# A graph layer on one core: layers in five parts, later merging, and 16 chunks loaded row by row instead of 21

## The chip, the cores and the metric

The kernel runs on one core of a Trainium2 chip. The metric is the time of one execution on the device in microseconds; lower is better. The core's engines work side by side, each through its own queue: PE multiplies matrices, DVE and ACT do elementwise work, POOL issues the indirect gathers, and SP (and in the set-up ACT) issues the plain transfers.

## The reference

One block of a graph network: normalise the rows of x, take the mean of the source rows over the edges that end at each node, and send mean and own row through four dense layers.

```python
h = jnp.maximum(_layernorm(x, axis=-1), 0.0)           # x: (12500, 128)
msgs = h[src]                                          # src, dst: (200000,), sorted by dst
agg = jax.ops.segment_sum(msgs, dst, num_segments=n)
deg = jax.ops.segment_sum(ones, dst, num_segments=n)
agg = agg / jnp.maximum(deg, 1.0)[:, None]
y = jax.nn.relu(agg @ Wg + h @ Ws + bg)                # 128
y = jnp.tanh(y @ W1 + b1)                              # 512
y = jnp.tanh(y @ W2 + b2)                              # 512
return x + (y @ W3 + b3)                               # 128
```

All of it is float32; the input has its edges sorted by dst.

## The kernel before

The program first normalises x in pieces of up to 14 x 128 rows and stores the result, the table `htab`, in HBM (lines 162 to 234). Meanwhile POOL gathers 80 chunks of rows straight from x ("raw" chunks, line 141), since the table isn't there yet; they are normalised later, eight at a time.

A chunk is 128 edges, 1563 chunks in all. For each, the 128 source rows must come into SBUF, and PE multiplies them with a one-hot matrix (which edge belongs to which node of a window of 56 to 160 nodes), adding up in PSUM: this is an add (`add`, line 413). There are three ways for the rows to come in:

- the 80 raw chunks, ten groups of eight, every 40 chunks from chunk 256 on;
- 1462 chunks by one indirect DMA each, issued by POOL (`gather`, line 296), into a ring of 32 buffers (`AHEAD`);
- 21 chunks row by row: SP reads each row's address into a register and issues a plain DMA of 512 bytes (`row_loads`, line 315). `slow` lists these chunks: from `SLOW0` = 72 up to `QUICK` = 1376, after each one `EACH` = 58 others that are not raw. They come in batches of 16 rows, a batch for every 58 x 16 / 128 = 7.25 gathered chunks, into two buffers. For each such chunk `places` (line 307) loads its 128 indices and DVE multiplies them by the length of a row, one chunk ahead.

The nodes are cut into blocks: 23 of 512, one of 256, three of 128 and one of 84. Blocks that share chunks have these added into a tensor of their own (`edge`), which is merged into both blocks' sums by a matmul with the identity (`merge`, line 437). Two chunks behind the last chunk of a block, `merge` runs and the block's layers start.

`layers` (line 498) is a generator; each `next` emits a matmul or so. Up to chunk `QUICK` the main loop (line 586) takes one step of the oldest block's layers every two chunks. From there on the order is timed: `there` (line 612) is a chunk's due time, 12.0 + 1.25 us for each gather, and before each add all steps are emitted that fit ahead of it; `soonest` (line 568) chooses between the two oldest blocks. PE's order is the program's order: `pe` and `sp_dma` keep what they issue in place.

The own rows of a block, `hb`, and x, `xb`, are loaded by `own` (line 460) some 50 chunks ahead; `own_turned` transposes `hb`. Sums, layers and x end in `o`, which SP stores `LATE` = 12 chunks later.

Of the kernel before, what the change touches and what calls it, by code (L numbers as in the profile page):

```python
# [22 lines left out]
F32 = mybir.dt.float32  # L23
BF16 = mybir.dt.bfloat16
I32 = mybir.dt.int32
U8 = mybir.dt.uint8
AF = mybir.ActivationFunctionType
ALU = mybir.AluOpType
# [10 lines left out]
RAW0 = 256  # L39
STEP = 40  # L40
AHEAD = 32
SLOW0 = 72
EACH = 58
LOADS = 16
LATE = 12
QUICK = 1376

WINDOWS = ((0, 144), (1496, 88), (1536, 56))
# [9 lines left out]
def windowed(ctx, tc, x, src, dst, Wg, Ws, bg, W1, b1, W2, b2, W3, b3, out, flag):  # L58
# [20 lines left out]
    def raw(c):  # L79
        return RAW0 <= c < RAW1 and (c - RAW0) % STEP < GRP  # L80


    slow, n = [], 0
    for c in range(SLOW0, QUICK):
        if not raw(c):
            if n == 0:
                slow.append(c)
                n = EACH
            else:
                n -= 1  # L90
# [202 lines left out]
    def sp_dma(*a):  # L293
        tc.keep_in_program_order(nc.sync.dma_start(*a))  # L294

    def gather(c):
# [4 lines left out]
        )  # L301
        rows_t[c] = r

    ROWB = 4 * D
    hbytes = htab.rearrange("n d -> (n d)").bitcast(U8)

    def places(c):

        ix = ed.tile([1, P], I32, name="ix", bufs=2)
        sp_dma(ix, src[c * P : (c + 1) * P].rearrange("(o p) -> o p", o=1))  # L310
        at = ed.tile([1, P], I32, name="at", bufs=2)
        nc.vector.tensor_scalar(at, ix, float(ROWB), None, op0=ALU.mult)
        return at

    def row_loads():
        nxt_at = places(slow[0])
        for i, c in enumerate(slow):
            at = nxt_at
            if i + 1 < len(slow):
                nxt_at = places(slow[i + 1])  # L320
            r = rows_one.tile([P, D], F32, name="srows")
            rows_t[c] = r
            rb = r.bitcast(U8)
            for p0 in range(0, P, LOADS):
                loads, vs = nc.values_load_multi_w_load_instructions(
                    at[:, p0 : p0 + LOADS], engines=[mybir.EngineType.SP], min_val=0, max_val=(N - 1) * ROWB,
                    skip_runtime_bounds_check_because="src holds rows of x, as the indirect DMAs take it to",
                )
                for ld in loads:
                    tc.keep_in_program_order(ld)  # L330
                for p, v in enumerate(vs, p0):
                    sp_dma(rb[p : p + 1, :], hbytes[bass.ds(v, ROWB)].rearrange("(o b) -> o b", o=1))
                yield
# [126 lines left out]
    def own(s):  # L460

        n0 = s * BLK
        n = min(BLK, N - n0)
        k, whole = -(-n // P), n // P
        xb = ml.tile([P, BLK // P, D], F32, name="xb", bufs=3)
        if whole < k:
            nc.vector.memset(xb[:, whole, :], 0.0)
        if whole:
            sp_dma(xb[:, :whole, :], x[n0 : n0 + whole * P, :].rearrange("(t p) d -> p t d", p=P))
        if whole < k:  # L470
            sp_dma(xb[: n - whole * P, whole, :], x[n0 + whole * P : n0 + n, :])
        hb = ml.tile([P, BLK // P, D], F32, name="hb", bufs=1)
        sp_dma(hb[:, :k], htab[n0 : n0 + k * P, :].rearrange("(t p) d -> p t d", p=P))
        owns[s] = (hb, xb)

    def own_turned(s):

        k = -(-min(BLK, N - s * BLK) // P)
        hb, xb = owns.pop(s)
        pt = ps_t.tile([P, BLK // P, P], F32, name="pt")  # L480
        for t in range(k):
            pe.transpose(pt[:, t, :], hb[:, t, :], ident)
        hT = ml.tile([P, BLK], F32, name="hT")
        nc.scalar.copy(hT[:, : k * P], pt[:, :k, :].rearrange("p t n -> p (t n)"))
        hTs[s] = (hT, xb)

    def own_part(b):

        n0, n = blocks[b]
        whole = n // P  # L490
        xb = ml.tile([P, -(-n // P), D], F32, name=f"xs{b}", bufs=1)
        if whole:
            sp_dma(xb[:, :whole, :], x[n0 : n0 + whole * P, :].rearrange("(t p) d -> p t d", p=P))
        if n > whole * P:
            sp_dma(xb[: n - whole * P, whole, :], x[n0 + whole * P : n0 + n, :])
        xss[b] = xb

    def layers(b):


        n0, n = blocks[b]
        s, off = divmod(n0, BLK)
        hT, xb = hTs[s]
        k, whole = -(-n // P), n // P
        rest = n - whole * P
        if n != BLK:
            xb = xss.pop(b)
        mm, hop = 4 * (n / 2400 + 0.003), 0.5 + n / 1200

        size, bufs = (P, 2) if n <= P else (BLK, 1)  # L510
        yield 0, 0
        mT = ml.tile([P, BLK], F32, name="mT")
        nc.vector.tensor_tensor(mT[:, :n], acc[b][:, :n], rds.pop(b)[:, :n], op=ALU.mult)  # L513
        yield mm, 0
        p0 = flat(ps_m.tile([P, 4, P], F32, name="pm"))
        pe.matmul(p0[:, :n], ws, hT[:, off : off + n], start=True, stop=False)
        yield mm, n / 90
        pe.matmul(p0[:, :n], wg, mT[:, :n], start=False, stop=True)
        h0 = ml.tile([P, BLK], F32, name="h0")
        nc.scalar.activation(h0[:, :n], p0[:, :n], AF.Relu, bias=bgc)  # L520
        yield 0, 0
        h1 = ml.tile([P, HM, size], F32, name=f"h1_{size}", bufs=bufs)
        for m in range(HM):
            yield mm, hop if m == 0 else 0
            p1 = flat(ps_m.tile([P, 4, P], F32, name="pm"))
            pe.matmul(p1[:, :n], w1[:, m * P : (m + 1) * P], h0[:, :n], start=True, stop=True)
            nc.scalar.activation(h1[:, m, :n], p1[:, :n], AF.Tanh, bias=b1c[:, m : m + 1])  # L527
        h2 = ml.tile([P, HM, size], F32, name=f"h2_{size}", bufs=bufs)
        for m in range(HM):
            p2 = flat(ps_m.tile([P, 4, P], F32, name="pm"))  # L530
            for kk in range(HM):
                yield mm, hop if m == 0 and kk == HM - 1 else 0
                pe.matmul(
                    p2[:, :n], w2[:, kk, m * P : (m + 1) * P], h1[:, kk, :n], start=(kk == 0), stop=(kk == HM - 1)
                )
            nc.scalar.activation(h2[:, m, :n], p2[:, :n], AF.Tanh, bias=b2c[:, m : m + 1])  # L536
        p3 = flat(ps_m.tile([P, 4, P], F32, name="pm"))
        for kk in range(HM):
            yield mm, hop if kk == HM - 1 else 0
            pe.matmul(p3[:, :n], w3[:, kk, :], h2[:, kk, :n], start=(kk == 0), stop=(kk == HM - 1))  # L540
        h3 = ml.tile([P, BLK], F32, name="h3", bufs=1)
        nc.scalar.activation(h3[:, :n], p3[:, :n], AF.Identity, bias=b3c)  # L542
        yield 0, 0
        yield k * 0.225, hop
        po = ps_t.tile([P, BLK // P, P], F32, name="pt")
        for t in range(k):
            r = min(P, n - t * P)
            pe.transpose(po[:r, t, :], h3[:, t * P : t * P + r], ident)
        o = ml.tile([P, BLK // P, D], F32, name="o")
        if whole:  # L550
            nc.vector.tensor_tensor(o[:, :whole], po[:, :whole], xb[:, :whole], op=ALU.add)
            stores.append((at, out[n0 : n0 + whole * P, :].rearrange("(t p) d -> p t d", p=P), o[:, :whole, :]))
        if rest:
            nc.vector.tensor_tensor(o[:rest, whole], po[:rest, whole], xb[:rest, whole], op=ALU.add)
            stores.append((at, out[n0 + whole * P : n0 + n, :], o[:rest, whole, :]))

    order = [c for c in range(NCH) if not raw(c) and c not in slow]
    loading = row_loads()
    work, done, nxt, behind = [], 0, 0, 0
# [6 lines left out]
            sp_dma(*stores.pop(0)[1:])  # L566

    def soonest():
        two = work[: 2 if len(work) > 1 and work[1][3] < work[0][3] else 1]
        return min(two, key=lambda w: max(w[2], now), default=None)  # L570

    def go_on(w):
        nonlocal now
        if w:
            now = max(now, w[2]) + w[1]
            w[1:] = *next(w[0], (None, 0)), w[3] + 1
            w[2] += now
            if w[1] is None:
                work.remove(w)
# [6 lines left out]
    for c in range(NCH):  # L586
# [22 lines left out]
                next(loading, 0)  # L609
        if c >= QUICK:  # L610

            there = 12.0 + 1.25 * (NRAW * GRP + order.index(c)) if c not in slow else 0
            while soonest() and max(now, soonest()[2]) < there:
                go_on(soonest())
            now = max(now, there) + 0.27
        add(c)

        if done < len(blocks) and (c - 2 if across[done] else c) == reach[done][-1]:
            if across[done]:
                merge(done)  # L620
            work.append([layers(done), 0, 0, 0])
            done += 1
        if (c // span + 1) * BLK < N:
            if c % span == span - 52:
# [389 lines left out]
```

## Time and profile before

| | us |
|---|---|
| median of 3 runs | 1955.35 (1953.97 to 1955.7) |
| profiled execution | 1952.27 |
| its span | 1950.5 |
| POOL busy | 1458.0 (75%) |
| PE busy | 1354.8 (69%) |
| DVE busy | 1069.7 (55%) |
| ACT busy | 231.8 (12%) |

The profile is that of one execution, with times from the start of its span. A group of instructions shows the line, the engine, the operation, the tile written and those read, the count, the busy time with the mean of one, and the engine's idle time ahead of them with what ended it. "issue" stands for time in which the engine waited for nothing that the profile shows. The records name line 285, 288 or 294 for all of PE's edge and layer matmuls, transposes and SP's plain DMAs, since helpers issue them; the tile names tell them apart. A float32 matmul appears as two records.

### The profile page before, as it was taken

To read this page: it belongs to the slowest core of one execution; us is meant where nothing else is said; L and a number is where in the kernel's file an instruction comes from. 1 tells how busy PE (TensorE), PEld (TensorE's weight loads), DVE (VectorE), ACT (ScalarE), POOL (GpSimd) and SP (SyncE) were. 2 spreads that over 40 slices of the span, in tenths; PEclk is the share of its full clock that TensorE was granted. 3 is DMA by queue.
4 is the path that set the end of the run, shared out by engine and by line. 5 is a ranking of instruction groups with operands and counts; after the bars stand their busy time and mean duration, and the time that the engine had idled before them with its cause. 6 is when DMAs were issued, how large, how long until landed. Compare 5 with 4: busy or idle time off the path is not lost.

```text
span 1950.5 us, 20753 instructions
## 1 busy us (share of the span) xinstructions
PE 1354.8 (69%) x5213; PEld 803.5 (41%) x5213; DVE 1069.7 (55%) x671; ACT 231.8 (12%) x364; POOL 1458.0 (75%) x1550
## 2 busy tenths in 40 slices
PE   0057387778787787776676677677776676778797
PEld 0034253444454444433333334343343343454466
DVE  7874874655666566645445445455455454545430
ACT  1100211101111011101011001010110101101122
POOL 7777777777777777777777777777777777777774
PEclk9999689899899989999999998989889889868797
DMA  7822222222222222222222222222222222222221
GB/s 199 231 77 65 54 70 54 70 65 60 71 70 71 64 60 70 70 54 71 70 54 70 54 71 70 54 71 65 60 70 54 71 70 53 77 69 61 55 63 38
DMA packets 125595, 139.78 MB, mean 72 GB/s; under 512 B 33169, under 2 KB 99958, under 8 KB 125272
## 3 DMA queue, kind: packets, MB, share of 16 engines
q0 software_dynamic: 49344, 101.16, 20.5%
q1 hardware_dynamic: 72962, 33.90, 6.3%
q10 hardware_dynamic: 3160, 3.31, 0.6%
q8 instruction: 43, 0.70, 0.2%
q14 instruction: 86, 0.70, 0.1%
HBM read 125.43 MB, written 12.82 MB: 71 GB/s over the span
## 4 chain that ended last, share of the span: by engine, by line
issue 36%; DMA 26%; PE 24%; POOL 11%; DVE 1%; ACT 0%; SPq 0%; POOLq 0%; DVEq 0%; ACTq 0%
DMA rows<-htab,scol 26%; PE pm L285 12%; PE agg L285 8%; POOL rows L298 7%; POOL raw L141 4%; PE edge L285 3%; PE pt L288 1%; DVE oh L362 0%; DVE shared L171 0%; DVE raw L172 0%; DVE shared L175 0%; ACT sq L174 0%; DMA raw<-in_x_dram,rsrc 0%; SPq L294 0%; DVE rd L399 0%
## 5 line engine op out<-in xcount | busy, mean ns | idle before, releaser
L298 POOL DMA_INDIRECT rows<-htab,scol x1462 | 1379.5, 944 | 445.8 <-issue 293.4
L285 PE MATMUL agg<-oh,rows 128*128 128x144 f32 (+3 forms) x2096 | 543.9, 358 | 331.5 <-DMA rows<-htab,scol 327.7
L285 PEld LDWEIGHTS agg<-oh,rows 128*128 128x128 f32 x2096 | 369.4, 217 | 711.4 <-DMA rows<-htab,scol 595.0
L285 PE MATMUL pm<-h,w 128*128 128x512 f32 (+3 forms) x1344 | 614.1, 553 | 0.2
L362 DVE TENSOR_TENSOR oh<-shared,dloc 128x1152 f32<-128x1152 f32 (+2 forms) x186 | 245.2, 1322 | 622.5 <-PE agg L285 420.3
L372 DVE TENSOR_REDUCE cnt<-oh 128x200 bf16<-128x1600 f32 (+2 forms) x186 | 523.6, 2825 | 7.9 <-DMA htab<-h 3.6
L285 PE MATMUL edge<-oh,rows 128*128 128x144 f32 (+2 forms) x828 | 211.9, 347 | 131.3 <-DMA rows<-htab,scol 130.4
L285 PEld LDWEIGHTS edge<-oh,rows 128*128 128x128 f32 x828 | 139.8, 206 | 264.6 <-DMA rows<-htab,scol 216.9
L285 PEld LDWEIGHTS pm<-h,w 128*128 128x128 f32 x1344 | 212.7, 197 | 11.8 <-issue 9.8
L536 ACT ACTIVATE h<-pm,b2c 128x512 f32<-128x512 f32 (+3 forms) x112 | 70.8, 632 | 649.1 <-PE pm L285 649.1
L141 POOL DMA_INDIRECT raw<-in_x_dram,rsrc x80 | 77.6, 970 | 25.5 <-issue 23.8
L527 ACT ACTIVATE h<-pm,b1c 128x512 f32<-128x512 f32 (+3 forms) x112 | 70.2, 632 | 182.1 <-PE pm L285 181.5
L399 DVE RECIPROCAL rd<-rd 128x512 f32<-128x512 f32 (+3 forms) x28 | 81.8, 2920 | 0.0
L513 DVE TENSOR_TENSOR mT<-agg,rd 128x512 f32<-128x512 f32 (+3 forms) x28 | 17.3, 619 | 90.5 <-PE agg L285 90.5
L200 PE MATMUL pm<-ident,idx_f 98*128 98x98 f32 x32 | 6.2, 376 | 76.3 <-DVE agg L179 42.7
L285 PE MATMUL agg<-sums,ident 128*128 128x140 f32 (+3 forms) x108 | 28.4, 412 | 27.5 <-ACT sums L427 27.5
L397 DVE TENSOR_SCALAR rd<-pm 128x512 f32<-128x512 f32 (+3 forms) x28 | 17.4, 621 | 52.4 <-PE pm L285 52.4
L520 ACT ACTIVATE h<-pm,bgc 128x512 f32<-128x512 f32 (+3 forms) x28 | 17.7, 632 | 236.4 <-PE pm L285 236.4
L542 ACT ACTIVATE h<-pm,b3c 128x512 f32<-128x512 f32 (+3 forms) x28 | 17.7, 632 | 184.5 <-PE pm L285 184.5
L285 PE MATMUL pm<-hT,ws 128*128 128x512 f32 (+3 forms) x56 | 38.6, 784 | 0.0
L285 PEld LDWEIGHTS agg<-sums,ident 128*128 128x128 f32 x108 | 25.4, 309 | 28.3 <-ACT sums L427 28.3
L200 PEld LDWEIGHTS pm<-ident,idx_f 98*128 98x128 f32 x32 | 5.1, 223 | 77.1 <-issue 42.9
(70 smaller groups left out, 497.4 us busy)
## 6 DMA issues: line engine op xcount, KB each, us to landing
srows<-htab SPq DMA_DIRECT2D x2688, 0.5 KB
rows<-htab,scol POOLq DMA_INDIRECT x1462
xb<-in_x_dram SPq DMA_DIRECT2D x24, 256.0 KB
hb<-htab SPq DMA_DIRECT2D x24, 256.0 KB
out_dram<-o SPq DMA_DIRECT2D x23, 256.0 KB
htab<-h SPq DMA_DIRECT2D x6, 896.0 KB
xt<-in_x_dram SPq DMA_DIRECT2D x5, 896.0 KB
raw<-in_x_dram,rsrc POOLq DMA_INDIRECT x80
```

The source lines that it names most:

```text
L141: nc.gpsimd.indirect_dma_start(out=t[:, j, :], out_offset=None, in_=x, in_offset=bass.IndirectOffsetOnAxis(ap=rsrc[:, g, j : j + 1], axis=0),)
L285: tc.keep_in_program_order(nc.tensor.matmul(*a, **k))
L288: tc.keep_in_program_order(nc.tensor.transpose(*a, **k))
L298: nc.gpsimd.indirect_dma_start(out=r, out_offset=None, in_=htab, in_offset=bass.IndirectOffsetOnAxis(ap=scol[:, c : c + 1], axis=0),)
L362: nc.vector.tensor_tensor(oh[:, :k, :w], lane[:, None, :w].to_broadcast([P, k, w]), dloc[:, g * GRP : g * GRP + k][:, :, None].to_broadcas ...
L372: nc.vector.tensor_reduce(cnt[:, :n], shifted, AX.X, ALU.add)
L397: nc.vector.tensor_scalar(rd[:, :m], dg[:, :m], 1.0, None, op0=ALU.max)
L399: nc.vector.reciprocal(rd[:, :m], rd[:, :m])
L520: nc.scalar.activation(h0[:, :n], p0[:, :n], AF.Relu, bias=bgc)
L527: nc.scalar.activation(h1[:, m, :n], p1[:, :n], AF.Tanh, bias=b1c[:, m : m + 1])
L536: nc.scalar.activation(h2[:, m, :n], p2[:, :n], AF.Tanh, bias=b2c[:, m : m + 1])
L542: nc.scalar.activation(h3[:, :n], p3[:, :n], AF.Identity, bias=b3c)
```

## The change

- **Layers in parts.** `layers` is split into `part0` (mean, first layer), `part1` and `part2` (the two tanh layers), `part3` (last matmul) and `part4` (transposes, adding x, store). For blocks whose layers start before `QUICK`, `part3` and `part4` of a block run within the next block's: `part0(b)`, `part3(b-1)`, `part1(b)`, `part4(b-1)`, `part2(b)`.
- **Merging.** Up to `QUICK` a block is merged, and its layers start, 10 chunks (`LEAD`) behind its last chunk instead of 2; after that 2 as before.
- **Row loads.** `SLOW0` goes from 72 to 160, `EACH` from 58 to 80, and the list ends at chunk 1462 instead of 1375. That makes 16 chunks (160, 241, ... 1375), and a batch of 16 rows for every 10 gathered chunks.
- **Their offsets.** The indices of all 16 chunks are loaded in the set-up by 16 DMAs on ACT's queue into 16 partitions and multiplied by one DVE instruction; `places` goes away.
- **x.** `own` loads only `hb`; x is loaded by `own_part` when a block's layers start.
- **The timed order.** The due time is 7.5 + 1.251 us for each gather; the second oldest block is chosen only if the oldest is one of the last small ones (`w[4]`).

```diff
-SLOW0 = 72
-EACH = 58
+SLOW0 = 160
+EACH = 80
 LOADS = 16
 LATE = 12
+LEAD = 10
 QUICK = 1376
...
-    for c in range(SLOW0, QUICK):
+    for c in range(SLOW0, NCH - 100):
...
-    def places(c):
-
-        ix = ed.tile([1, P], I32, name="ix", bufs=2)
-        sp_dma(ix, src[c * P : (c + 1) * P].rearrange("(o p) -> o p", o=1))
-        at = ed.tile([1, P], I32, name="at", bufs=2)
-        nc.vector.tensor_scalar(at, ix, float(ROWB), None, op0=ALU.mult)
-        return at
+    at_i = const.tile([len(slow), P], I32, name="at_i")
+    for i, c in enumerate(slow):
+        nc.scalar.dma_start(at_i[i : i + 1, :], src[c * P : (c + 1) * P].rearrange("(o p) -> o p", o=1))
+    place = const.tile([len(slow), P], I32, name="place")
+    nc.vector.tensor_scalar(place, at_i, float(ROWB), None, op0=ALU.mult)
...
     def row_loads():
-        nxt_at = places(slow[0])
         for i, c in enumerate(slow):
-            at = nxt_at
-            if i + 1 < len(slow):
-                nxt_at = places(slow[i + 1])
...
-                    at[:, p0 : p0 + LOADS], engines=[mybir.EngineType.SP], min_val=0, max_val=(N - 1) * ROWB,
+                    place[i : i + 1, p0 : p0 + LOADS], engines=[mybir.EngineType.SP], min_val=0, max_val=(N - 1) * ROWB,
...
+    def one_by_one(*parts):
+        for part in parts:
+            yield from part()
+
+    def layers(b, before):
+
+
+        part = lambda f, *a: lambda: f(*a)
+        last = [] if before is None else [part(part3, before), part(part4, before)]
+        if reach[b][-1] + LEAD < QUICK:
+            return one_by_one(
+                part(part0, b), *last[:1], part(part1, b, True), *last[1:], part(part2, b)
+            )
+        return one_by_one(
+            *last, part(part0, b), part(part1, b, False), part(part2, b), part(part3, b), part(part4, b)
+        )
...
     def soonest():
-        two = work[: 2 if len(work) > 1 and work[1][3] < work[0][3] else 1]
+        two = work[: 2 if len(work) > 1 and work[1][3] < work[0][3] and work[0][4] else 1]
...
-            there = 12.0 + 1.25 * (NRAW * GRP + order.index(c)) if c not in slow else 0
+            there = 7.5 + 1.251 * (NRAW * GRP + order.index(c)) if c not in slow else 0
...
-        if done < len(blocks) and (c - 2 if across[done] else c) == reach[done][-1]:
+        lead = LEAD if c < QUICK else 2
+        if done < len(blocks) and (c - lead if across[done] else c) >= reach[done][-1]:
             if across[done]:
                 merge(done)
-            work.append([layers(done), 0, 0, 0])
+            quick = reach[done][-1] + LEAD >= QUICK
+
+            before = done - 1 if done and reach[done - 1][-1] + LEAD < QUICK else None
+            work.append([layers(done, before), 0, 0, 0, quick and blocks[done][1] <= P])
             done += 1
```

The bodies of the five parts are those of the old `layers`, cut at these places; `part0` calls `own_part` for a block of 512, and `part1` gives two empty steps more before `QUICK`.

## The prediction

> **What bounds the kernel now.** I read the groups of the page first, then POOL's own waits, then the timeline at both ends of POOL's gathers.
>
> ```profile
> L298 POOL DMA_INDIRECT rows<-htab,scol x1462 | 1379.5, 944 | 445.8 <-issue 293.4
> L285 PE MATMUL agg<-oh,rows 128*128 128x144 f32 (+3 forms) x2096 | 543.9, 358 | 331.5 <-DMA rows<-htab,scol 327.7
> L285 PE MATMUL edge<-oh,rows 128*128 128x144 f32 (+2 forms) x828 | 211.9, 347 | 131.3 <-DMA rows<-htab,scol 130.4
> ```
>
> POOL issues 1462 gathers of 944 ns and is idle 445.8 us between them; PE sits idle some 460 us ahead of its adds, waiting for gathered rows. Whether POOL ever waits for something is told by the longest wait of each kind (last column):
>
> ```profile
> POOL rows L298 <- issue: 293.4, 962, 0.3
> POOL rows L298 <- PE agg L285: 61.0, 200, 0.3
> POOL rows L298 <- DMA rows<-htab,scol: 35.4, 116, 0.3
> POOL rows L298 <- PE edge L285: 27.1, 89, 0.3
> ```
>
> None is over 0.3 us, whatever engine it is booked to: this is the fixed gap of a gather (445.8 / 1462 = 0.305 us), not a stall. So the page's 75% busy POOL is saturated. The two ends of the row of gathers, on POOL's timeline:
>
> ```profile
> 103.70 0.94 POOL L141 DMA_INDIRECT raw<-in_x_dram,rsrc  x1 [0.30 <-issue]
> 104.94 0.95 POOL L298 DMA_INDIRECT rows<-htab,scol  x1 [0.30 <-issue]
> ...
> 1928.98 0.94 POOL L298 DMA_INDIRECT rows<-htab,scol  x1 [0.31 <-POOLq L980]
> ```
>
> (1928.98 - 104.94) / 1461 = 1.2485 us for a gather, and the 80 raw gathers run straight into the first table gather. The kernel is POOL from 2.95 to 1928.98, then a tail of 1950.5 - 1928.98 = 21.5 us. A chunk of 128 edges that SP loads row by row costs POOL nothing; a gathered one costs 1.2485 us.
>
> **The count of gathers (on the path).** There are 1563 chunks (200000 / 128), 80 raw. Before, from chunk 72 to 1375 there are 1304 - 80 = 1224 that are not raw; one of 59 is row-loaded, 21 in all, so 1563 - 80 - 21 = 1462, as the page counts. After, from 160 to 1462 there are 1303 - 80 = 1223; one of 81 is row-loaded, 16 in all, so 1467. Five more gathers: 5 x 1.2485 = +6.24 us, on the engine that never waits.
>
> **What is taken from SP and DVE.** SP issues 5 x 128 = 640 fewer row DMAs, 21 fewer index loads and 40 fewer register loads (168 to 128). Sixteen row DMAs took 5.65 us of SP at 107.67, so a batch now fills 5.65 of 10 x 1.2485 = 12.5 us instead of 5.65 of 7.25 x 1.2485 = 9.1. Does POOL speed up? From 1300 to 1610, with row loads running, its gathers stand 1.2483 us apart; from 1630 to 1930, after the last row load at 1619, also 1.2483. So 0. The first two row chunks fill both buffers either way; later a batch waits for the add that frees its buffer, and behind it on SP queue x, table and output transfers. Each chunk is loaded 80 gathers ahead of its add by program order (160 - 80) where it was 14 (72 - 58): 100 us of cover against 17.5. Nothing.
>
> DVE loses 21 multiplies:
>
> ```profile
> L312 DVE TENSOR_SCALAR at<-ix x21: 158/204/370, 106.0 to 1497.1; 1x128 int32<-1x128 int32 x21
> 106.20 0.99 POOL L298 DMA_INDIRECT rows<-htab,scol  x1 [0.30 <-issue]
> 29.18 1.21 DVE L196 CAST idx_f<-idx_raw 98x2048 f32<-98x2048 int32 x1
> 29.32 1.90 POOL L141 DMA_INDIRECT raw<-in_x_dram,rsrc  x1 [0.30 <-issue]
> ```
>
> The gather beside the first two multiplies took 0.99 instead of 0.94; no other of the 1462 is above that (its longest is 990 ns). One wide multiply comes instead, beside a raw gather: 0.05 gone, 0.05 back, at most its 0.2 us. I take 0. The cast does cost the gather beside it 0.96 us; both casts stay. The Trainium skill, SBUF — State Buffer, section "SBUF: two separate sides", says that a VectorE operation in a two-port mode locks GpSimd out for the whole instruction. If that held for the multiplies too, their removal would save 21 x 0.217 = 4.6 us and the sum would be +1.6 instead of +6.2; the row of the cast fits the rule, the row of the multiplies doesn't, and the row decides.
>
> **Set-up.** ACT's queue gets 16 DMAs more, behind b3c. The eight bias loads before them began 0.52 us apart (28.71 to 32.37), so 16 x 0.52 = 8.3 us. Eleven stand ahead of the square that started at 37.81 with 5.1 us of empty queue before it: 11 x 0.52 = 5.7, so it is 0.6 late; five stand after it, 2.6 us beside its 1.70 us and the 2.17 us that ACT then waited for DVE. Behind them queue the dst index load and the next factors, and DVE's wide multiply waits for all 16. That is between 0 and 8.3 - 5.1 = 3.2 us late; if the last five also wait for a store of 640 KB (the last table store took from 93.2 to 98.1, 4.9 us), 8.1. The cover:
>
> ```profile
> 98.17 0.50 SPq L294 DMA_DIRECT2D hb<-htab  x1
> ```
>
> This load needs the whole table, which is there by 98.1; the first gather starts at 104.94 because POOL is still at raw gathers. So 6.8 us of lateness cost nothing, and the worst is 8.1 - 6.8 = +1.3. DVE, 60.5 of 63 us busy from 30 to 93, sets the end of the table; in the changed order three one-hots of 1.35 us come behind its last piece, which gives 4 us back. I take 0.
>
> **Layers in five parts, merge 10 chunks ahead.** The matmuls, tanhs and transposes are the same in number; only their places among the adds change, in the stretch where PE idles for rows. That makes PE wait less for ACT, and then wait longer for rows: 0. The cover is the ring of 32 row buffers, 32 x 1.2485 = 40 us: POOL is held only when PE falls that far behind. The longest stretch of layers without an add stands where the timed order starts, at chunk 1376: 36 records, 15.6 us (1698.48 to 1714.1). In the changed order some 42 records stand there, 15.6 x 42 / 36 = 18.2 us. Even at half clock this is 36.4, under 40. x is now loaded a block ahead of its use; no one waits.
>
> **The tail.** Behind the last wide blocks, the changed PE order is the same as before, matmul for matmul, over the last 25 adds and all layers of blocks 25 to 27 among and behind them: the constants 7.5 and 12.0 shift all due times alike. So I carry 21.5 us over. Its bounds:
>
> ```profile
> 1931.43 0.49 PE L285 MATMUL agg<-oh,rows 128*128 128x44 f32 x2
> 1934.28 0.30 PE L285 MATMUL agg<-oh,rows 128*128 128x28 f32 x2
> 1934.62 0.24 DVE L513 TENSOR_TENSOR mT<-agg,rd 128x84 f32<-128x84 f32 x1 [9.00 <-PE agg L285]
> 1943.91 0.29 DVE L554 TENSOR_TENSOR o<-pt,xs 84x128 f32<-84x128 f32 x1 [6.12 <-PE pt L288]
> ```
>
> Then busy time of PE, PE's loads, DVE, ACT and POOL in stretches of 2 us, with the granted clock behind them:
>
> ```profile
> 1920.00:1922.00 2.00, 0.84 (x4) 0.59 (x4) 0.00 (x0) 0.00 (x0) 1.46 (x2) 1.00 0.18 43
> 1922.00:1924.00 2.00, 0.85 (x7) 0.70 (x6) 0.26 (x2) 0.24 (x1) 1.39 (x3) 0.50 0.21 55
> ...
> 1930.00:1932.00 2.00, 2.00 (x11) 2.00 (x11) 0.00 (x0) 0.33 (x1) 0.00 (x0) 0.50 0.13 33
> 1932.00:1934.00 2.00, 2.00 (x18) 2.00 (x18) 0.00 (x0) 0.73 (x2) 0.00 (x0) 0.94 0.00 0
> ```
>
> A gather's rows reach PE 2.54 us after its start (the chain's commonest piece), the last ones at 1931.5; the last add ran at 1934.28, since PE was at half clock from 1922 to 1932. With PE in time the tail loses 2.8 us at most. The other way: at half clock to the very end, PE's 11.2 us of work from 1932 to 1944 would take up to 11 longer; both half-clock stretches (1902 to 1911.8, 1922 to 1932) ended some 7.5 us after PE was dense, so I take 0, and 2 for the range (4 us more at half speed). The Trainium skill, TensorE: Matmul & The Clock Gate, section "Part 1: The HAM clock gate (the "warmup" mystery)", gives a free-running window of 3.4 us; by an estimate from that page 6.24 us of shift could move the change of clock by a window, 1.7 us of work either way. Here half clock went on for 7 us after PE was dense (1904.1 to 1911.8).
>
> **Sum.** The profiled execution took 1952.27 us (span 1950.5 and 1.8 around it); 1952.27 + 6.24 = 1958.5. The median of the runs is 1955.35, 3.1 above it: 1955.35 + 6.24 = 1961.6, +0.32%. I call 0.2% (3.9 us) the least that a measurement of this kernel can tell from no change.
>
> **Rivals.**
> - The tail gives it back: better timed, PE reaches the last add with its rows. Price up to -2.8 us, 1958.8; it decides from 6.24 - 3.9 = 2.3 us on, not slower then. For it speaks the 2.8 us lag of the last add; against it the order of matmuls, unchanged there. 0.12.
> - Set-up or ring becomes the bound: the table lands after the last raw gather, or PE falls 40 us behind. +1.3 by the first, some us by the second, 1963 to 1966. Against both the covers above, 6.8 us and 22 us. 0.06.
> - The change doesn't do it by gathers: lighter SP and DVE make each gather shorter, so that 1467 of them take less. Faster needs (6.24 + 3.9) / 1467 = 0.007 us off each of them; the two equal intervals of 1.2483 speak against it. 1951.5 or less. 0.04, of which 0.03 faster.
> - The forecast, 1961.6: 0.78.
>
> Slower: 0.78 + 0.06 = 0.84. Same: 0.12 + 0.01 = 0.13. Faster: 0.03. The range runs from the tail's bound, 1958.5, to the set-up's 1.3 and the clock's 2 above the forecast with a us for the spread of runs, 1966.
>
> **What would show it.** Right: 1467 gathers in the groups, no wait of POOL over 0.3 us, first table gather at 105, last at 1935.2, and 21.5 us behind it. Wrong: a gap on POOL ahead of the first table gather (set-up), waits of POOL for PE over 0.3 us (ring), another interval than 1.2485 (rate), or a tail away from 21.5 us.

## The result and the profile after

| | before | after |
|---|---|---|
| median of 8 runs, us | 1955.34 (1953.97 to 1956.59) | 1960.88 (1960.20 to 1961.69) |
| ratio, with its 95% interval | | 1.0028 (1.0017 to 1.0039) |
| profiled execution, us | 1952.27 | 1961.69 |
| its span | 1950.5 | 1959.5 |
| gathers by POOL | 1462 | 1467 |
| first, last table gather starts at | 104.94, 1928.98 | 104.73, 1938.59 |
| from the last gather to the end | 21.5 | 20.9 |

The change costs 5.54 us, 0.28%; the interval of the ratio, 1.0017 to 1.0039, leaves out 1. One slip in the section on the change: the 16 row-loaded chunks run from 160 to 1455, not to 1375, since the raw chunks between them are skipped in the count.

The groups of the page of after first; the columns are those of the groups shown of before:

```profile
L299 POOL DMA_INDIRECT rows<-htab,scol x1467 | 1387.6, 946 | 447.5 <-issue 269.3
L286 PE MATMUL agg<-oh,rows 128*128 128x144 f32 (+3 forms) x2096 | 560.2, 365 | 335.2 <-DMA rows<-htab,scol 324.3
```

Five gathers more, and PE still idles 335 us ahead of the adds of `agg`, for rows. POOL's waits of after, with the longest of each kind last:

```profile
POOL rows L299 <- issue: 269.3, 883, 0.3
POOL rows L299 <- PE agg L286: 74.4, 244, 0.3
POOL rows L299 <- DMA rows<-htab,scol: 47.9, 157, 0.3
POOL rows L299 <- PE edge L286: 29.3, 96, 0.3
```

None is longer than the fixed gap of 0.3 us: POOL runs through, as before. The ends of its row of gathers, on POOL's timeline:

```profile
103.48 0.95 POOL L142 DMA_INDIRECT raw<-in_x_dram,rsrc  x1 [0.31 <-issue]
104.73 0.95 POOL L299 DMA_INDIRECT rows<-htab,scol  x1 [0.30 <-DVE cnt L367]
...
1938.59 0.95 POOL L299 DMA_INDIRECT rows<-htab,scol  x1 [0.30 <-POOLq L1014]
```

(1938.59 - 104.73) / 1466 = 1.2509 us a gather, against 1.2485 before. Over 1466 intervals this is 3.5 us, over half of what the five gathers cost; the two profiles by themselves therefore differ by 9.0 us of span where the medians differ by 5.5. Whether the 1.2509 belongs to the change had to be asked with a second execution (below: it doesn't). The eight timed runs of before lie 3.1 us above its profiled one in the median (1955.34 against 1952.27), close to these 3.5 us, so the slower pace may have held for both kernels in the timed runs; no profile shows it.

### The profile page after: what moved, and what is told of

It is laid out like the page before. It is cut to its first block, busy times and chain, and to the rows that moved or that the text cites. A ratio compares the mean times of both kernels' runs of the same rounds, so it can differ in the third digit from the quotient of the medians.

```text
span 1959.5 us, 19291 instructions
## 1 busy us (share of the span) xinstructions
PE 1393.8 (71%) x5213; PEld 824.1 (42%) x5213; DVE 1068.2 (55%) x650; ACT 231.8 (12%) x364; POOL 1465.9 (75%) x1555
## 4 chain that ended last, share of the span: by engine, by line
DMA 36%; issue 28%; PE 26%; POOL 7%; DVE 3%; ACT 0%; SPq 0%; ACTq 0%; POOLq 0%; DVEq 0%
DMA rows<-htab,scol 34%; PE pm L286 13%; PE agg L286 9%; POOL rows L299 7%; PE edge L286 3%; DMA xt<-in_x_dram 2%; PE pt L289 1%; DMA at_i<-in_src_dram 0%; DVE oh L357 0%; DVE agg L176 0%; DVE h L183 0%; DVE agg L172 0%; DVE xt L173 0%; DVE cnt L367 0%; DVE shared L176 0%
## 5 line engine op out<-in xcount | busy, mean ns | idle before, releaser
L286 PE MATMUL agg<-oh,rows 128*128 128x144 f32 (+3 forms) x2096 | 560.2, 365 | 335.2 <-DMA rows<-htab,scol 324.3
L286 PEld LDWEIGHTS agg<-oh,rows 128*128 128x128 f32 x2096 | 381.9, 223 | 714.1 <-DMA rows<-htab,scol 597.5
L286 PE MATMUL pm<-h,w 128*128 128x512 f32 (+3 forms) x1344 | 639.0, 573 | 1.1 <-ACT h L515 0.7
L286 PEld LDWEIGHTS edge<-oh,rows 128*128 128x128 f32 x838 | 145.0, 210 | 277.1 <-DMA rows<-htab,scol 242.3
L286 PEld LDWEIGHTS pm<-h,w 128*128 128x128 f32 x1344 | 219.8, 202 | 15.2 <-issue 12.0
L564 DVE TENSOR_TENSOR o<-pt,xb 128x512 f32<-128x512 f32 x23 | 15.9, 690 | 95.7 <-PE pt L289 91.9
L472 ACT COPY hT<-pt 128x512 f32<-128x512 f32 (+1 forms) x25 | 14.4, 578 | 258.5 <-PE pt L289 246.9
L289 PE MATMUL pt<-ident,hb 128*128 128x128 f32 x98 | 16.6, 297 | 31.5 <-DMA srows<-htab 31.5
```

The source lines that it names most:

```text
L286: tc.keep_in_program_order(nc.tensor.matmul(*a, **k))
L289: tc.keep_in_program_order(nc.tensor.transpose(*a, **k))
```

## The experiments

The experiments ran on three chips, and each is compared only with the kernel before on its own chip. There before took 2498.71 us (first group below), 1951.77 (second group; 1951.51 beside the last run, on the same chip) and 1952.18 (third group). The chip of the first group is slower, SP's queue among the rest, for a cause that stays open.

### On a slow chip

*again* is the kernel before, unchanged, for its profile on this chip.

> The kernel before, unchanged, for its trace beside the others. After the change a gather took 1.2509 us in the profile, before it 1.2485. If the change makes gathers slower, this run shows 1.2485 again and the change's 1466 intervals hold 3.5 us that the count doesn't explain. If the two executions differ as a whole, it shows 1.250 to 1.251 here, with raw gathers at the same distance.

*count16* is the kernel before with the changed numbers of row loads alone: 16 chunks instead of 21, and nothing else of the change.

```diff
-SLOW0 = 72
-EACH = 58
+SLOW0 = 160
+EACH = 80
...
-    for c in range(SLOW0, QUICK):
+    for c in range(SLOW0, NCH - 100):
```

> The kernel before with 16 row-loaded chunks, 80 gathers apart, and nothing else of the change. Theory (each gathered chunk costs its 1.25 us on POOL): 1467 gathers, 5 x 1.25 = +6.25 us, about 1961.6. Rival (the layers in parts and the later merging cost the 5.5 us, the count is free): within 1 us of 1955.3.

*back21* is the changed kernel with the same lines set back, so 21 chunks and all the rest of the change.

> The changed kernel with the old 21 chunks, 58 gathers apart; layers, merging, timed order and offsets as changed. Theory: 1462 gathers, 1960.9 - 6.25 = 1954.6, within 1 us of the kernel before. Rival (layers and merging cost it): stays near 1960.9.

*more26* is the changed kernel with `SLOW0` = 88 and `EACH` = 50, so 26 chunks.

> The changed kernel with 26 row-loaded chunks, 50 gathers apart, from chunk 88 on. Theory: 1457 gathers, 1960.9 - 10 x 1.25 = 1948.4, 0.35% below the kernel before. Rival (SP is the bound of row loads): a batch of 16 rows takes SP some 6.3 us when it never waits, and comes every 50 x 16 / 128 x 1.25 = 7.8 us here; if SP's other transfers and waits push it over, PE waits for row-loaded chunks, POOL waits for PE, and the time is above 1952.

| kernel | row-loaded chunks | us, median | ratio to before, interval |
|---|---|---|---|
| before | 21 | 2498.71 (17 runs) | |
| again | 21 | 2505.59 (1 run) | |
| count16 | 16 | 2311.61 (5 runs) | 0.9261 (0.9234 to 0.9288) |
| back21 | 21 | 2483.63 (12 runs) | 0.9954 (0.9925 to 0.9984) |
| more26 | 26 | 2635.14 (5 runs) | 1.0556 (1.0523 to 1.0588) |

Everything is turned round here: fewer row loads are faster, more are slower. SP's timeline and POOL's waits of *again* say why, and then SP's register moves, one ahead of each row load (shortest, median and longest in ns):

```profile
600.19 14.36 SPq L294 DMA_DIRECT2D srows<-htab  x13
614.60 0.41 SPq L294 DMA_DIRECT2D out_dram<-o  x1
616.91 22.50 SPq L294 DMA_DIRECT2D srows<-htab  x31
```

```profile
POOL rows L298 <- issue: 337.6, 1017, 18.7
POOL rows L298 <- PE agg L285: 261.9, 154, 21.2
POOL rows L298 <- PE edge L285: 119.2, 70, 14.6
```

```profile
L294 SPq MOVE srows<-htab x2150: 2/29/1411, 300.2 to 1899.8; - x196
```

Here SP needs 14.36 / 13 = 1.10 and 22.50 / 31 = 0.73 us for a row load (the second stretch holds a register load), where 16 of them took 5.65 us (0.353 each) in the profile of before. The median move takes 29 ns, as in *after*, but single ones take up to 1.41 us; in *after* the longest between 300 and 1900 us is 37 ns. POOL now has waits of up to 21 us for PE: an add stands in PE's queue until its rows are in, PE falls behind by the whole ring of 32 buffers, and POOL stops. Between 16 and 21 row chunks each one costs (2498.71 - 2311.61) / 5 = 37.4 us here instead of saving 1.25.

SP isn't all that is slow on this chip. Behind SP's last row load, at 2163.5 us, the gathers of *again* still stand (2459.48 - 2203.77) / 171 = 1.495 us apart:

```profile
L298 POOL DMA_INDIRECT rows<-htab,scol x172: 941/947/957, 2203.8 to 2459.5; - x172
```

In *count16* they stand (2263.46 - 115.82) / 1466 = 1.465 us apart from the first to the last. At that pace 16 row chunks leave SP 80 x 1.465 = 117 us each, and 21 leave it 58 x 1.465 = 85; SP took 95 us for one in *again* (2150 row loads in 1600 us). So SP is the bound there with 21 and 26 chunks and not with 16, and the slower pace of the gathers themselves, by estimate 1467 x (1.465 - 1.2485) = 318 us, has a cause of its own that no run shows. What was expected of these runs was made for an ordinary chip and is missed; the changed kernel itself was not run here.

### The change, its count alone, and more row loads

*after2* is the changed kernel as it is, *count16b* is *count16* again, and *more26b* is *more26* again.

> The changed kernel, unchanged, beside the kernel before on the same chip. On the chip of the first comparison it took 1.0028 of the time before. On chip 3, where the kernel before took 2499 us and its SP queue moved a register in up to 1.41 us instead of 0.029, 16 row-loaded chunks alone brought the time to 0.926. If this run falls on a chip like the first, the theory (five more gathers) says 1.0025 to 1.0032; on a chip like chip 3, row loads are what bounds, and it says about 0.92.

> The kernel before with 16 row-loaded chunks, 80 gathers apart, as in count16, again. On a chip where the kernel before takes 1955: theory +6.25 us, 1961.6; rival (layers and merging cost the 5.5 us) within 1 us of 1955.3. On a chip where it takes some 2500: 0.926 again, and within 1% of the changed kernel, since the count is what differs.

> The changed kernel with 26 row-loaded chunks, 50 gathers apart, as in more26, again. On a chip where the kernel before takes 1955: theory 1457 gathers, 1948.4; rival (SP falls behind at 7.8 us for a batch) above 1952. On a chip where it takes some 2500: 1.05 again, bound by SP.

| kernel | gathers | us, median | ratio to before, interval |
|---|---|---|---|
| before | 1462 | 1951.77 (15 runs) | |
| after2 | 1467 | 1957.13 (10 runs) | 1.0026 (1.0016 to 1.0035) |
| count16b | 1467 | 1958.53 (6 runs) | 1.0033 (1.0021 to 1.0045) |
| more26b | 1457 | 1943.75 (5 runs) | 0.9958 (0.9945 to 0.9972) |

The count alone costs +6.76 us, and the whole change +5.36: the five gathers account for the loss. The rest of the change seems to give 1.4 us back: the intervals overlap (1.0016 to 1.0035 against 1.0021 to 1.0045), but every run of *count16b* (1957.85 and up) lies above every run of *after2* (1957.58 at most). Which part of the change gives it isn't shown. POOL's timeline of *after2* at its two ends:

```profile
104.47 0.94 POOL L299 DMA_INDIRECT rows<-htab,scol  x1 [0.30 <-issue]
...
1934.59 0.94 POOL L299 DMA_INDIRECT rows<-htab,scol  x1 [0.30 <-PE pm L286]
```

(1934.59 - 104.47) / 1466 = 1.2484 us. The interval of 1.2509 in the first profile is thus one of that execution, or chip, not of the change; *count16b*, without the rest of it, ran at 1.2499. The span of 1955.1 against the 1950.5 of before splits into -0.5 ahead of the first table gather, +6.1 for the gathers (1830.12 against 1824.04) and -1.0 behind the last one.

### What covers what

The four runs of this group fell on one chip, where before took 1952.18 us. The changed kernel itself was not run there; *loads48* and *pecut* have one run each.

*loads48* issues the 16 index loads three times.

```diff
-    for i, c in enumerate(slow):
-        nc.scalar.dma_start(at_i[i : i + 1, :], src[...])
+    for t in (at_j, at_k, at_i):
+        for i, c in enumerate(slow):
+            nc.scalar.dma_start(t[i : i + 1, :], src[...])
```

> The changed kernel with its 16 index loads issued three times over (48 small transfers on ACT's queue, into three tensors; only the last is multiplied). It asks how much lateness of the set-up is covered. In the changed kernel 16 loads took 11.4 us of ACT's queue (0.71 us each), and the table's first reader (hb) was at 98.76 us, 6 us ahead of the first table gather at 104.73. Theory (the last table piece waits for ACT's queue, the cover is 6 us): 32 x 0.71 = 22.7 us more on that queue. If ACT's work of the set-up is pushed back whole, the table is 17 to 22 us later, the first table gather stands at 115 to 121, POOL shows a gap of 10 to 16 us ahead of it, and the time is as much longer. Rival (ACT has slack, DVE sets the end of the table): the first table gather within 1 us of 104.7 and the time unchanged.

1956.12 us (one run), 3.9 above before, where the changed kernel was 5.4 and 5.5 above it on the other chips. The theory fell: the first table gather didn't move. Of its profile, the ACT queue's timeline, DVE's, SP's and POOL's, a line or two each:

```profile
64.78 5.48 ACTq L313 DMA_DIRECT2D at_i<-in_src_dram  x7
70.36 1.70 ACT L175 ACTIVATE sq<-xt 128x1792 f32<-128x1792 f32 x1 [12.45 <-DMA at_i<-in_src_dram]
94.51 0.21 DVE L315 TENSOR_SCALAR place<-at_i 16x128 int32<-16x128 int32 x1
99.76 0.38 SPq L295 DMA_DIRECT2D hb<-htab  x1
104.27 0.94 POOL L299 DMA_INDIRECT rows<-htab,scol  x1 [0.30 <-issue]
```

A square stands 12.45 us behind the loads, and yet `hb`, the table's first reader, is at 99.76 against 98.76 in the changed kernel, and the first table gather at 104.27. The work on DVE came out in another order: the multiply `place` went from 49.66 to 94.51, behind the last piece of the table, and DVE did other pieces while ACT was held. So ACT being late by more than the 6 us between 98.76 and 104.73 is not yet a late table: DVE had other work to go on with. From which lateness on it would be one wasn't tried.

*pecut* uses one of the four parts of W2 in blocks whose layers run among the adds.

```diff
+            last = 0 if reach[b][-1] + LEAD < QUICK else HM - 1
...
+                if kk > last:
+                    continue
```

> The changed kernel with three quarters of the matmuls of the second tanh layer left out for the blocks whose layers run among the adds (one of four 128x128 pieces of W2 is used, so those outputs are another function). Work of some 200 us leaves PE. It asks whether PE's work in the long middle sets anything. Theory (POOL's gathers set the pace, PE's place and amount of work is free there): first table gather, interval (1.2484 to 1.251 us) and the time of the last gather within 1 us of those of the changed kernel's fixed pace, 1467 gathers, the tail within 1 us; time within 2 us of the changed kernel on the same chip (before + 5.5). Rival (PE bounds it in places): up to 200 us less, at least some us less.

1956.06 us (one run), 3.9 above before, as *loads48*. The group of the tanh layers' matmuls in the page of *pecut*, then POOL's longest waits for PE in it:

```profile
L286 PE MATMUL pm<-h,w 128*128 128x512 f32 (+3 forms) x840 | 414.9, 600 | 1.3 <-ACT h L515 1.1
```

```profile
POOL rows L299 <- PE agg L286: 99.4, 326, 0.3
POOL rows L299 <- PE edge L286: 44.8, 147, 0.3
```

In the changed kernel this group is x1344 and 639.0 us, so 224 us of matmuls are gone, and the gathers from first to last took 1830.20 us against 1830.12 in *after2*. These matmuls set nothing at POOL. Little of their time is freed: the mean granted clock falls from 0.901 to 0.788, the adds of `agg` take 618.6 us instead of 560.2, and PE's busy time in all falls by only 36 us (1393.8 to 1358.2).

*filler* keeps PE busy in the last 60 chunks.

```diff
+        if c >= NCH - 60 and not work:
+            for _ in range(3):
+                pe.matmul(shared[:, W_MAX : W_MAX + NROW], ident, ident[:, :NROW], ...)
```

> The changed kernel with three matmuls of 128x128 by 98 columns, into columns of PSUM that nobody reads, ahead of each add of the last 60 chunks where no layer's steps are due. It asks whether half clock of PE near the end costs anything in the tail (the prediction's bound: 2.8 us at most). Theory A (half clock makes the last add late): with PE kept busy the granted clock stays at 1 ahead of the last gather, the last add starts 2.5 to 3.5 us behind the last gather instead of 5.1, and the time is 1.5 to 2.8 us below the changed kernel's (before + 2.6 to 4.0). Theory B (the tail is set by what comes in last whatever the clock, or the extra matmuls delay as much as they help): time within 1 us of the changed kernel's, before + 4.5 to 6.5.

1956.32 us (9 runs, 1955.17 to 1965.72), ratio 1.0031 (1.0020 to 1.0042). That is 4.14 us above before, between theory A's 2.6 to 4.0 and theory B's 4.5 to 6.5, and within 0.3 us of *loads48* and *pecut*: the time shows no gain. The profile shows that A's mechanism is there all the same. In stretches of 2 us, the granted clock third from the end: first the changed kernel, whose last gather starts at 1938.59, then *filler*, with its last gather at 1934.86:

```profile
1938.00:1940.00 2.00, 2.00 (x12) 2.00 (x11) 0.00 (x0) 1.30 (x4) 1.23 (x2) 0.50 0.16 39
1940.00:1942.00 2.00, 2.00 (x11) 2.00 (x11) 0.00 (x0) 0.33 (x1) 0.00 (x0) 0.50 0.18 41
1942.00:1944.00 2.00, 2.00 (x20) 2.00 (x19) 0.00 (x0) 0.49 (x3) 0.00 (x0) 1.00 0.00 0
```

```profile
1930.00:1932.00 2.00, 1.86 (x16) 1.58 (x14) 1.13 (x5) 0.11 (x1) 1.70 (x2) 1.00 0.25 66
1934.00:1936.00 2.00, 1.98 (x18) 1.78 (x17) 0.00 (x0) 0.66 (x2) 1.49 (x2) 1.00 0.25 70
```

The clock stays at 1 in *filler*. PE's last adds, of the changed kernel and of *filler*:

```profile
1943.72 0.30 PE L286 MATMUL agg<-oh,rows 128*128 128x28 f32 x2
```

```profile
1937.75 0.41 PE L286 MATMUL agg<-oh,rows 128*128 128x28 f32 x2
```

That is 5.13 and 2.89 us behind the last gather. Put in order by the end of half clock (read in stretches of 0.5 us), the profiled runs on ordinary chips (*more36*, a stalled one, aside) give one picture:

| run | half clock ends, behind the last gather | last add, behind it | from the last gather to the end |
|---|---|---|---|
| filler | none | 2.89 | 18.34 |
| loads48 | 0.5 | 3.88 | 19.39 |
| pecut | 1.0 | 3.92 | 19.57 |
| more26b | 1.0 | 4.06 | 19.66 |
| count16b | 2.0 | 4.52 | 20.21 |
| after2 | 2.5 | 4.67 | 20.51 |
| after | 3.5 | 5.13 | 20.91 |
| before | 3.5 | 5.30 | 21.52 |
| more29 | 4.0 | 5.97 | 21.44 |

The tail is no constant: where the half clock happens to end decides some 2 us of it, and *loads48* and the changed kernel, with the same work there, stand 1.5 apart. Filler matmuls take half clock out, and some 1.1 us of the tail against *loads48* and *pecut* on the same chip. That this shortens the median isn't shown: five of the nine runs lie at 1955.2 to 1956.3, where *loads48* and *pecut* have 1956.1, the other four higher, one by 9 us.

The clock changes only on a fixed grid. In *before* it changes at 1901.5, 1911.8, 1922.0, 1932.3 and 1945.9 us, in *filler* at 1913.4, 1916.8 and 1951.0, and in all nine profiles any two changes in a row lie a whole multiple of 3.41 us apart (here 3, 3, 3 and 4 times, and 1 and 10 times). Where the grid falls against the last gather differs from run to run. Read exactly, half clock ends 0.7 to 4.2 us behind it in the eight profiles, a spread of about one step. The steps before and behind the change at 1932.26 in *before*, in the columns of the stretches above:

```profile
1928.85:1932.26 3.41, 3.41 (x18) 3.41 (x17) 0.00 (x0) 1.30 (x4) 0.94 (x1) 0.50 0.15 41
1932.26:1935.67 3.41, 3.41 (x33) 3.41 (x32) 0.24 (x1) 1.17 (x4) 0.00 (x0) 1.00 0.00 0
```

*more29* loads 29 chunks row by row.

```diff
-SLOW0 = 160
-EACH = 80
+SLOW0 = 80
+EACH = 44
```

> The changed kernel with 29 chunks loaded row by row instead of 16 (from chunk 80, one of 45), so 1454 gathers, 13 fewer. A batch of 16 row loads every 44 x 16 / 128 = 5.5 gathers, 6.9 us; with its register loads it takes SP 6.3 us. Theory (gathers alone count as long as SP keeps up): 13 x 1.2485 = 16.2 us less than the changed kernel, about before - 10.8, and some 3.7 us less than with 26 chunks. Rival (SP's queue, now 92% full, is late with rows, tables and stores): POOL waits for PE because the ring of 32 is full, and the time is above that of 26 chunks, in the worst case above before.

1942.71 us (5 runs), ratio 0.9950 (0.9937 to 0.9964): 9.5 us below before, and faster than both kernels. The step from 26 chunks (0.9945 to 0.9972 on another chip) lies within the intervals. Its last gather:

```profile
1919.36 0.94 POOL L299 DMA_INDIRECT rows<-htab,scol  x1 [0.30 <-issue]
```

From the first one at 105.04 this is 1814.32 us, 15.8 less than in *after2* (13 gathers: 16.2). The gain by the time is smaller than the 10.8 expected; the first table gather stands 0.6 later than in *after2* and the tail, whose half clock ends latest of all, is 0.9 longer.

### Where SP ends

*more36* has `SLOW0` = 64 and `EACH` = 36.

> The changed kernel with 36 chunks loaded row by row (from chunk 64, one of 37), so 1447 gathers, 20 fewer than in the changed kernel. A batch of 16 row loads every 36 x 16 / 128 = 4.5 gathers, 5.6 us, while SP took 6.2 to 6.4 us for a batch with its register loads where 26 chunks were loaded. Theory 1 (SP has a limit at about 6.3 us a batch and becomes the bound): its 36 x 8 = 288 batches need some 288 x 6.3 = 1814 us and the x, table and output transfers besides, against 1447 x 1.2485 = 1807 us of gathers; batches fall behind, a row chunk's add waits for its rows, PE falls behind by more than the 32 buffers and POOL waits for PE: time above that of 29 chunks (before - 9.5), and POOL's interval above 1.26 us late in the row. Theory 2 (only gathers count): 20 x 1.2485 = 25.0 us below the changed kernel, about before - 18 to - 21, interval 1.2485. If the chip's SP queue is slow, as once, the time lies far above before and the run tells only that.

2193.36 us (4 runs, one of them far off at 3863.74) against 1951.51, ratio 1.1234 (1.1210 to 1.1259): theory 1, with a fall much harder than the step from 29 to 36 suggests. POOL's waits of *more36*, then POOL's and PE's timelines around one of its gaps, then SP's timeline, its register loads (shortest, median and longest in ns), and its longest wait from 620 to 1700 us:

```profile
POOL rows L299 <- PE agg L286: 271.6, 254, 14.3
POOL rows L299 <- PE edge L286: 98.3, 113, 11.9
```

```profile
1119.51 0.94 POOL L299 DMA_INDIRECT rows<-htab,scol  x1 [0.30 <-issue]
1129.36 0.94 POOL L299 DMA_INDIRECT rows<-htab,scol  x1 [8.91 <-PE agg L286]
...
1127.76 0.85 PE L286 MATMUL agg<-oh,srows 128*128 128x144 f32 x2 [30.30 <-DMA srows<-htab]
...
611.01 18.64 SPq L295 DMA_DIRECT2D srows<-htab  x48
...
L320 SPq TENSOR_LOAD <-place x288: 1136/1255/1857, 96.9 to 2046.0; - x144
...
SPq L295 <- PE agg L286: 0.8, 4, 0.3
```

PE stood 30.30 us at one add for rows that SP hadn't loaded (`srows`); as it got on, the buffers came free and POOL's next gather started, 8.91 us late. The gaps recur once for each row chunk: from the one at 1119.51 to the tenth after it at 1663.45, (1663.45 - 1119.51) / 10 = 54.4 us. That is what SP needs for a row chunk with everything else on its queue, for in this stretch SP never waits longer than 0.3 us (in *after* up to 38.2). The 18.64 us hold 48 row loads and the two register loads between their batches. By themselves a row load takes 0.33 us and a register load, with the gap around it, 1.33: 128 x 0.33 + 8 x 1.33 = 52.9, and x, tables and stores are the rest. POOL offers `EACH` x 1.2485: 44.9 us with 36, 54.9 with 44, 72.4 with 58 and 99.9 with 80. By this sum 44 is the last that fits, by half a us. The loss follows from the same numbers: the mean interval is (2169.94 - 104.65) / 1446 = 1.4283, so 1446 x (1.4283 - 1.2485) = 260 us of waiting, less 15 gathers saved (18.7) gives +241; measured +241.9.

## Why the prediction was right

**The count of gathers.** +6.24 us from five gathers on an engine that never waits: right. *count16b* has +6.76 from the count alone, *after2* +6.1 between its first and last gather, and *more26b* and *more29* shorten that stretch by 1.24 and 1.22 us for each gather fewer. Forecast 1961.6, measured 1960.88.

**The layers in five parts, 0.** Right within the 1.4 us between *count16b* and *after2*, and *pecut* shows that 224 us of layer matmuls can go without a trace at POOL. The ring's cover held; POOL has no wait over 0.3 us.

**SP lighter, 0.** Right on the ordinary chips, with a reason that was too generous. The prediction set a batch's 5.65 us against 9.1; with register loads and the other transfers on the queue a batch takes 54.4 / 8 = 6.8. Enough with 44 to 80 gathers between row chunks, and no longer with 36. The second rival, that the ring becomes the bound, has its place there and on the slow chip, not in this change on an ordinary chip.

**The set-up, 0.** The sum is right, its working isn't: the 16 loads took 11.4 us of ACT's queue, 0.71 each, where 0.52 had been carried over from the bias loads. ACT's and DVE's lines of the changed kernel, and SP's:

```profile
33.92 8.66 ACTq L310 DMA_DIRECT2D at_i<-in_src_dram  x11
42.63 1.70 ACT L175 ACTIVATE sq<-xt 128x1792 f32<-128x1792 f32 x1 [12.40 <-DMA at_i<-in_src_dram]
42.65 2.75 ACTq L310 DMA_DIRECT2D at_i<-in_src_dram  x5
49.66 0.38 DVE L312 TENSOR_SCALAR place<-at_i 16x128 int32<-16x128 int32 x1 [1.19 <-DMA at_i<-in_src_dram]
98.76 0.38 SPq L295 DMA_DIRECT2D hb<-htab  x1
```

The square came 4.8 us later than before instead of 0.6 (37.81 to 42.63), and DVE waited 1.19 us; the table's first reader moved from 98.17 to 98.76 (97.49 in *after2*). The cover was called DVE's own length and 6.8 us of raw gathers; *loads48* shows that it is wider still.

**The casts.** They were said to stay as they were. The gather beside the second took 1.57 us in the changed kernel against 1.96 before, but 1.97 in *more29* and 1.42 in *loads48*: these tenths, and the first table gather between 104.27 and 105.04, vary from run to run without an order by kernel.

**The tail, carried over at 21.5.** This step was mis-sized: 20.9 and 20.5 in two executions of the changed kernel, for which the first rival (up to -2.8 us) had the right place. Its reason was off: it isn't the order's due times but the phase of half clock that decides, and across all runs it moves the tail between 19.4 and 21.5, down to 18.3 without half clock. Of the medians the whole miss is 0.7 us (1961.6 against 1960.88). The tail's 0.6 in the first profile of the changed kernel is of that size, but no run shows that it is the cause. The prediction's estimate from the Trainium skill (TensorE: Matmul & The Clock Gate, section "Part 1: The HAM clock gate (the "warmup" mystery)"), that a shift against a free-running window of 3.4 us could move the end by 1.7 us either way, is near the 2.1 us between 19.4 and 21.5. The profiles agree on the window: the clock changes only on a grid of 3.41 us.

**The rate.** Rival three wanted each gather 0.007 us shorter. The interval was 1.2484 to 1.2509 in nine profiles, with 16 to 29 row chunks; 1.2484 in *after2* is the 1.2485 of before. By the prediction's own signs the first profile spoke against it (1.2509, and the last gather at 1938.59 instead of 1935.2); *after2*, at 1934.59, takes that back.

## What to carry to other kernels

Where one engine never waits, count its instructions: 5 x 1.25 us told the result, and the split layers, another merge point and the set-up told nothing. Work moved to a second queue to spare the first is free only up to that queue's own period, with everything on it counted (54.4 us for a row chunk, not 128 x 0.353 = 45.2); just within it lie the best versions (26 and 29 row chunks, 0.4 and 0.5% faster than before), beyond it a loss of 12% (36 row chunks, 44.9 us apart), and on a slower chip the limit lies elsewhere. A change of some tenths of a per cent is read from medians on one chip, not from two profiles: pace and tail of single executions differ by as much.

## What the hardware showed unexpectedly

- On one chip SP needed 0.73 to 1.10 us for a row load instead of 0.33 to 0.35, the gathers stood some 1.5 us apart even behind the last row load, and the kernel before took 2498.71 us instead of 1951 to 1955. Why is open.
- The clock changed only on a grid of 3.41 us, and where that grid fell against the last gather moved the tail by 2.1 us.
- The interval of gathers held 1.2484 to 1.2487 in seven profiles and was 1.2499 and 1.2509 in two, throughout the run.
- With PE's work cut, its granted clock fell (0.901 to 0.788), and what was left of it ran longer (the adds of `agg` 618.6 us instead of 560.2); of 224 us taken out, 36 came off its busy time.
